# Tying the last slab's scans behind its neighbour's norm, and copying the gate's projection out of its bank

## The chip, the cores and the metric

The kernel runs on one core of a Trainium2 chip. A core has a matrix engine (TensorE, PE in the profile), a vector engine (VectorE, DVE), a scalar engine (ScalarE, ACT), a general engine (GpSimd, POOL), and queues that issue DMA transfers (SyncE, SP, issues nearly all of them here). Each engine works through its own instructions in order, and engines wait for one another by semaphores. Matrix results land in PSUM, here in banks of 128 x 512 f32. The metric is device time of one execution, in microseconds. Before the change the median of three runs was 1083.98 us (1078.87 to 1085.02).

## The reference

Four layers run one after the other on x, 32 sequences of 64 rows of 256 numbers: a cross attention (L0), two transformer blocks (L1 and L2: self attention, cross attention, MLP), and a recurrent layer (L3). The change touches L3 alone. Its core, cut:

```
xn = ln(x); sx = token_shift(xn)                 # row before minus this row
x5 = xn + sx * (maa_stack + tanh((xn + sx*maa_x) @ maa_w1) @ maa_w2)   # five mixes
w = exp(-exp(time_decay + tanh(x5[1] @ decay_w1) @ decay_w2))
r, k, v = x5[3] @ Wr.T, x5[0] @ Wk.T, x5[2] @ Wv.T
g = silu(x5[4] @ Wg.T)
step: a = k v^T; out = r (u*a + s); s = a + w*s   # scan over the 64 rows
att = group_norm(out) * gn_w + gn_b               # mean and variance over 8 numbers
x = x + (att * g) @ Wo.T
xn2 = ln(x); ...; x = x + sigmoid(xr @ ffn_Wr.T) * (square(relu(xk @ ffn_Wk.T)) @ ffn_Wv.T)
```

## The kernel before

The rows stand in four groups of 512 (`NG`); x stays in SBUF as four tiles `x0` to `x3`. Every layer is written as a list of small Python closures ("pieces"), each with a due time; `emit` sorts the pieces of all lists by due time and runs them. That gives a priority to each instruction. A scheduler then lays out the five engines' orders, with a timeline of its own, from these priorities and from the buffers that come free. So the order on an engine isn't written by hand, and a small edit can move instructions that it doesn't name.

The recurrent layer works in eight slabs of 256 rows (`recurrent(n)`, n = 0 to 7, names ending in r0 to r7). The second half of L2's MLP (`mlp_half`, L556, names with L2m) is spread between the first slabs. A slab has three lists:

- `first`: layer norm and shift (`norm`, L619), the five mixes (`mix`, L676: PE into `px5`, DVE L689, POOL adds at L692), then projections. `project` (L700) takes a bank of the tag "mm", of which there are two, and fills it with four matmuls (eight in the profile's records): `pv` for values, `pr` for receptance (L729 copies it out), `pk` for keys (L736 multiplies it by the receptance into `rk`, a tile with one buffer), `pg` for the gate. `own_term` (L738) has PE read `rk` into `pcf`. `decay_b` leaves the decays in `wsh`.
- `second`: the recurrence, in two halves e = 0 and 1 of four columns each. `spread` (L721) has SP load the values, broadcast, into a 1 MB tile `vb`, from a ring of three buffers of the tag "big", which the MLP's `hT` shares. `outer` multiplies by the keys (DVE L782), `scan` (L794) runs four scans on DVE (L797), `read` multiplies by the receptance (DVE L782 again), `over_keys` sums on PE into `pa`. Then the group norm: `norm_a` (L813) adds the own term (L815), has PE average into `pgm`, subtracts the mean on DVE (L819, the centring) and squares on ACT (L821); `norm_b` (L823) has PE average the squares into `pgv`, takes Ln and Exp on ACT (L829, L830, each behind a table load), and four DVE instructions (L833, L834) apply the norm, the weights and the gate to `at`. `to_rows` multiplies by Wo into `pwo`, and L198 adds to x.
- `third`: layer norm (names with fr), mixes `xk` and `xr` (L652), `pkk`, `pfr` and `pfv` on PE, and the output.

The gate before the change: ACT takes tanh of the bank `pg` (L772), and DVE reads the same bank for the product (L773). So the bank is free when DVE has come to L773:

```
ps = project("Wg", st["x5", 4], "g")
nc.scalar.activation(gt, ps, AF.Tanh, scale=0.5)
nc.vector.scalar_tensor_tensor(gt, gt, 1.0, ps, ALU.add, ALU.mult)
```

Which instruction waits for which bank is fixed when the program is built. In this one, the first matmul of `pr` of slabs 1, 2, 3 and 4 waits for L773 of the slab before; those of slabs 5, 6 and 7 wait for ACT's copy of `pv` (L712).

Of the kernel before, what the change touches and what calls it, by code (L numbers as in the profile page):

```python
# [1 line left out]

# [16 lines left out]
ALU = mybir.AluOpType  # L19
# [4 lines left out]
P = 128  # L24
NG = 4
# [55 lines left out]
def tile_xattn_stack(ctx: ExitStack, tc: tile.TileContext, a: dict, out: bass.AP):  # L81
    nc = tc.nc
# [11 lines left out]
    def bank(name, tag="mm"):  # L94
        return psum.tile([P, 512], FP, tag=tag, name=name, bufs=BUFS[tag])
# [503 lines left out]

    RB, RR = GB // 2, GR // 2  # L600

    def recurrent(n, pool, c3):

        g, u = n // 2, n % 2
        t = f"r{n}"
        st = {}
        mine = slice(n * RB, (n + 1) * RB)

        def flat(ap):
            return ap.rearrange("p c b t -> p (c b t)")  # L610
# [5 lines left out]
        def tile_(name, bufs=2, shape=None, p=pool, tag=None):  # L616
            return p.tile(shape or [P, 2, RR], FP, tag=tag or name, name=f"{name}_{t}", bufs=bufs)

        def norm(key, scale, bias, tag, row_of_state):  # L619


            def evac(ps):
                xn = st[key] = pool.tile([P, 2, RR], FP, tag=key, bufs=2, name=f"xn_{tag}")
                for c in range(2):
                    nc.scalar.activation(
                        xn[:, c], ps[:, c], AF.Identity, bias=vec(bias, c), scale=vec(scale, c),
                    )

            def evac_step(ps):
                sx = st["d" + key] = pool.tile([P, 2, RB, S], FP, tag="d" + key, name=f"sx_{tag}", bufs=2)  # L630
                for c in range(2):
                    nc.scalar.activation(
                        sx[:, c].rearrange("p b t -> p (b t)"), ps[:, c], AF.Identity,
                        bias=tiny[:, 2:3], scale=vec(scale, c),
                    )
                nc.gpsimd.tensor_tensor(
                    sx[:, :, :, 0], c3["st01"][:, :, mine, row_of_state],
                    st[key].rearrange("p c (b t) -> p c b t", b=RB)[:, :, :, 0], ALU.subtract,
                )

            layernorm_T(
                6 if key == "x" else 7, g, u, tag, evac, None, "tp" if key == "fx" else "sc", "n" + key, pool, 1,
                (c3["step"], evac_step),
            )
# [55 lines left out]
        def project(w, x, name, tag="mm"):  # L700
            ps = both(f"p{name}_{t}", tag)
            for o in range(2):
                project_T(ps[:, o], c3[w], slice(o * P, (o + 1) * P), x)
            return ps
# [63 lines left out]
        def gate():  # L768

            gt = st["gt"] = tile_("gt")  # L770
            ps = project("Wg", st["x5", 4], "g")
            nc.scalar.activation(gt, ps, AF.Tanh, scale=0.5)  # L772
            nc.vector.scalar_tensor_tensor(gt, gt, 1.0, ps, ALU.add, ALU.mult)  # L773

        first = [(0.5, lambda: norm("x", "L3_ln1_w", "L3_ln1_b", t, 1)), (0.0, first_mix), (1.2, maa)]
        first += [(0.85, lambda: mix(2, 3)), (1.7, vals), (0.85, lambda: mix(0, 1)), (1.7, recept), (1.7, keys)]
# [16 lines left out]

        def scan(e):  # L794
            v = st["vb", e].rearrange("p d c t -> p d (c t)")
            for d in range(4):
                nc.vector.tensor_tensor_scan(v[:, d], flat(st["wsh"]), v[:, d], 0.0, ALU.mult, ALU.add)  # L797
            if e == 1:
                st["wdone"]()

# [12 lines left out]
        def norm_a():  # L813
            at = st["at"] = tile_("at")
            nc.vector.tensor_tensor(at, st["own"], st["pa"], ALU.add)  # L815
            ps = bank(f"pgm_{t}", "pc")[:, :RR]
            for c in range(2):
                nc.tensor.matmul(ps, c3["avg"], at[:, c], start=(c == 0), stop=(c == 1))
            nc.vector.tensor_tensor(at, at, ps.unsqueeze(1).broadcast_to([P, 2, RR]), ALU.subtract)  # L819
            st["sq"] = tile_("sq", 1)  # L820
            nc.scalar.activation(st["sq"], at, AF.Square)  # L821

        def norm_b():  # L823
            at, sq = st["at"], st["sq"]
            ps = bank(f"pgv_{t}", "pc")[:, :RR]
            for c in range(2):
                nc.tensor.matmul(ps, c3["avg"], sq[:, c], start=(c == 0), stop=(c == 1))

            nc.scalar.activation(ps, ps, AF.Ln, bias=tiny[:, 1:2])  # L829
            nc.scalar.activation(ps, ps, AF.Exp, scale=-0.5)  # L830
            gnh = c3["gnh"]
            for c in range(2):
                nc.vector.scalar_tensor_tensor(at[:, c], at[:, c], gnh[:, c : c + 1], ps, ALU.mult, ALU.mult)  # L833
                nc.vector.scalar_tensor_tensor(  # L834
                    at[:, c], at[:, c], gnh[:, 2 + c : 3 + c], st["gt"][:, c], ALU.add, ALU.mult
                )

        def to_rows(src, w, done, name):
            def part(v):
                if v == 0:  # L840
                    st[name] = bank(f"p{name}_{t}", "pc" if w == "Wo" else "tp").rearrange("p (j n) -> p j n", j=2)
                for c in range(2):
                    nc.tensor.matmul(  # L843
                        st[name][:, v], src()[:, c, v * P : (v + 1) * P], c3[w][:, c],
                        start=(c == 0), stop=(c == 1),
                    )
                if v == 1:
                    done(st[name])

            return [(0.85, lambda v=v: part(v)) for v in range(2)]  # L850

        second = []
# [38 lines left out]
        third = [(0.5, ff_norm), (0.0, ff_mix), (1.7, ff_key)]  # L891
        third += to_rows(lambda: st["xr"], "ffn_Wr", done_r, "fr")
        third += to_rows(lambda: st["kk"], "ffn_Wv", done_v, "fv")
        return first, second, third


    wts, c3 = {}, {}
# [20 lines left out]
    with tc.tile_pool(name="lw", bufs=1) as wp, tc.tile_pool(name="lp", bufs=2) as pool:  # L918
# [148 lines left out]
        def loads(pieces, t0, t1):  # L1067
            return timed([(1.0, p) for p in pieces], t0, t1)

        plan = [timed(layer0(pool), *L0_AT), loads(load_self("L1"), L0_LOAD, L0_LOAD + 2.0)]  # L1070
        late = []
        for i, L in enumerate(("L1", "L2")):
            for k in range(2):
                for g in range(NG):
# [5 lines left out]
                    at = (8 + GAP) * i + 4 * k + g  # L1080
# [4 lines left out]
            at = (8 + GAP) * i + MLP  # L1085
# [17 lines left out]
    with tc.tile_pool(name="r", bufs=2, reuse_waits="tile") as pool:  # L1103
        def load(name, shape, src):
            load_to(pool, name, shape, src)

        def load_w(*names):
            for n in names:
                load(n, [P, 2, E], a["w3"][W3[n]].rearrange("(c p) n -> p c n", p=P))

        def hold(tag, bufs=2, shape=None):
            pool.tile(shape or [P, 2, RR], FP, tag=tag, name=f"hold_{tag}", bufs=bufs)

        def shifted_ring(name):

            c3[name] = ring(pool, name, [P, 2, RB, S], 2, lambda t: nc.gpsimd.memset(t[:, :, :, 0], 0.0))

        hold("fx")
        hold("dfx")
        hold("x5", 3)  # L1120
        hold("nx", 1)
        shifted_ring("wsh")
        hold("xk")
        hold("xr")
        hold("kk")
        hold("x")
        hold("rr", 2, [P, 2, E])
        hold("dx")
        shifted_ring("vsh")
        hold("ta", 1, [P, RR + S])  # L1130
        hold("vT")
        hold("rT")
        hold("tb", 1, [XM, RR])
        hold("rk", 1)
        hold("dT", 1, [64, RR])
        selu = c3["selu"] = pool.tile([P, 2, P], FP, name="selu", bufs=1)
        load_w("Wg", "Wo", "ffn_Wk", "ffn_Wr", "ffn_Wv")
        load("s0", [P, 2, RS, B], a["s0"])
        hold("gt")
        hold("at")  # L1140
        hold("sq", 1)
        shifted_ring("ksh")
        hold("nfx", 1)
        for c in range(2):
            nc.vector.tensor_scalar(selu[:, c], c3["sel"][:, c], vec("L3_faaaa", c), None, ALU.mult)
        gnh = c3["gnh"] = pool.tile([P, 4], FP, name="gnh", bufs=1)
        for i, n in enumerate(("L3_gn_w", "L3_gn_b")):
            nc.vector.tensor_scalar(
                gnh[:, 2 * i : 2 * i + 2], vecs[:, VEC[n] : VEC[n] + 2], 0.5, None, ALU.mult
            )  # L1150
        r = [recurrent(n, pool, c3) for n in range(2 * NG)]
        plan = []
        for n, (first, second, third) in enumerate(r):
            at = n * SLOT + START
            plan += [timed(first[:1], at - LEAD, at - LEAD), timed(first[1:], at, at + R1_D)]
            at += R2
            plan += [timed(second, at, at + R2_D)]
            at += R2_D + F0
            plan += [timed(third[:1], at, at), timed(third[1:], at + F1, at + F1 + F1_D)]
        plan.append(late)  # L1160
        emit(*plan)
# [78 lines left out]
```

## Time and profile before

The profile is of one execution, which took 1080.68 us; its span, first instruction to last, is 1078.9 us. All times below count from the start of that span.

| what | value |
|---|---|
| median of three runs | 1083.98 us |
| profiled execution, its span | 1080.68 us, 1078.9 us |
| PE, DVE, ACT, POOL busy | 983.6, 806.2, 549.2, 532.2 us |
| mean granted TensorE clock | 0.962 |
| 750 to 900 us: PE, DVE, ACT busy of 150 | 132.7, 127.4, 69.9 us |
| 900 to 1025 us: PE, DVE, ACT busy of 125 | 114.3, 113.3, 57.5 us |
| 1025 to 1079 us: PE, DVE, ACT busy of 54 | 35.7, 33.2, 22.8 us |
| scans L797 in the recurrent layer | 64, 77.6 us, 1276 ns each |

The recurrent layer's gates run from 749 us (slab 0) to 1027 us (slab 7). A share of busy time is an average: what a change is worth is read where its instructions stand, from the waits there. The timeline has, for each engine, the start and length of instructions, in brackets how long the engine had been idle, and what ended that. "PEclk" is the granted clock of PE as a share of full speed.

### The profile page before, as it was taken

To read this page: it belongs to the slowest core of one execution; us is meant where nothing else is said; L and a number is where in the kernel's file an instruction comes from. 1 tells how busy PE (TensorE), PEld (TensorE's weight loads), DVE (VectorE), ACT (ScalarE), POOL (GpSimd) and SP (SyncE) were. 2 spreads that over 40 slices of the span, in tenths; PEclk is the share of its full clock that TensorE was granted. 3 is DMA by queue.
4 is the path that set the end of the run, shared out by engine and by line. 5 is a ranking of instruction groups with operands and counts; after the bars stand their busy time and mean duration, and the time that the engine had idled before them with its cause. 6 is when DMAs were issued, how large, how long until landed. Compare 5 with 4: busy or idle time off the path is not lost.

```text
span 1078.9 us, 26319 instructions
## 1 busy us (share of the span) xinstructions
PE 983.6 (91%) x10764; PEld 787.8 (73%) x10764; DVE 806.2 (75%) x1513; ACT 549.2 (51%) x1271; POOL 532.2 (49%) x552
## 2 busy tenths in 40 slices
PE   8998999899989999989989999898989898988966
PEld 4886776667778989877767778787768677765645
DVE  5864688878877654777787887647887987999983
ACT  4743653554456644864454555454436464453334
POOL 4343766767657344756577665442434434153200
PEclk9999998999999999989899999999889999998889
DMA  9300111111100100140111101112122121332400
GB/s 301 105 21 21 23 45 32 38 25 27 26 22 7 40 1 21 46 138 22 41 39 28 26 21 32 31 36 66 41 70 60 50 61 40 95 76 69 98 11 29
DMA packets 45947, 53.39 MB, mean 49 GB/s; under 512 B 16146, under 2 KB 40068, under 8 KB 43780
## 3 DMA queue, kind: packets, MB, share of 16 engines
q1 hardware_dynamic: 40292, 49.60, 17.1%
q10 hardware_dynamic: 5536, 2.12, 0.8%
q8 instruction: 85, 1.39, 0.5%
q14 instruction: 34, 0.28, 0.1%
HBM read 38.83 MB, written 4.21 MB: 40 GB/s over the span
## 4 chain that ended last, share of the span: by engine, by line
PE 43%; DVE 32%; ACT 8%; POOL 8%; issue 4%; DMA 3%; SPq 0%; ACTq 0%; POOLq 0%; DVEq 0%
DVE vb_r L797 6%; PE pf_L1m L187 4%; PE pf_L2m L187 3%; DVE vb_r L782 3%; PE pfo_L1m L187 3%; POOL s_L2c L463 2%; DVE x L198 2%; POOL s_L1c L463 2%; PE pr L312 2%; PE pfo_L2m L187 2%; PE pwo_r L843 1%; PE px_r L132 1%; PE pq_L1c L187 1%; DVE s_L1c L458 1%; POOL s_L1s L463 1%
## 5 line engine op out<-in xcount | busy, mean ns | idle before, releaser
L692 POOL TENSOR_TENSOR x_r<-x_r,xn_r 128x512 f32<-128x512 f32 x40 | 63.6, 1604 | 113.7 <-DVE x_r L689 111.8
L797 DVE TENSOR_TENSOR_SCAN vb_r<-wsh,vb_r 128x512 f32<-128x512 f32 x64 | 77.6, 1276 | 5.6 <-ACT wsh L696 4.1
L463 POOL TENSOR_TENSOR s_L1s<-s_L1s,n 128x512 f32<-128x512 f32 x32 | 43.0, 1356 | 39.9 <-DVE s_L1s L458 39.2
L187 PE MATMUL pf_L2m<-lnT_L2m,w_L 128*128 128x256 f32 x384 | 57.8, 303 | 1.7 <-ACT vbd L430 0.7
L187 PEld LDWEIGHTS pf_L2m<-lnT_L2m,w_L 128*128 128x128 f32 x384 | 51.8, 202 | 7.6 <-issue 2.5
L187 PE MATMUL pfo_L2m<-w_L,hT_L2m 128*128 128x256 f32 x384 | 55.2, 291 | 1.5 <-DVE hT_L2m L581 1.5
L463 POOL TENSOR_TENSOR s_L2s<-s_L2s,n 128x512 f32<-128x512 f32 x32 | 43.0, 1360 | 26.9 <-DVE s_L2s L458 26.3
L187 PE MATMUL pfo_L1m<-w_L,hT_L1m 128*128 128x256 f32 x384 | 54.5, 288 | 1.6 <-POOL hT_L1m L580 0.8
L187 PE MATMUL pf_L1m<-lnT_L1m,w_L 128*128 128x256 f32 x384 | 51.9, 288 | 3.9 <-ACT hf_L1m L577 1.2
L463 POOL TENSOR_TENSOR s_L2c<-s_L2c,n_L2c 128x512 f32<-128x512 f32 x32 | 41.6, 1320 | 27.6 <-DVE s_L2c L458 26.7
L463 POOL TENSOR_TENSOR s_L1c<-s_L1c,n_L1c 128x512 f32<-128x512 f32 x32 | 41.3, 1309 | 25.8 <-DVE s_L1c L458 24.8
L187 PEld LDWEIGHTS pf_L1m<-lnT_L1m,w_L 128*128 128x128 f32 x384 | 47.5, 191 | 7.2 <-ACT hf_L1m L577 2.1
L187 PEld LDWEIGHTS pfo_L2m<-w_L,hT_L2m 128*128 128x128 f32 x384 | 48.7, 190 | 5.2 <-issue 2.7
L187 PEld LDWEIGHTS pfo_L1m<-w_L,hT_L1m 128*128 128x128 f32 x384 | 49.3, 191 | 3.4 <-POOL hT_L1m L580 1.0
L580 POOL TENSOR_SCALAR hT_L1m<-hf_L1m 128x512 fp32r<-128x512 f32 x32 | 21.8, 682 | 55.4 <-ACT hf_L1m L577 53.5
L577 ACT ACTIVATE hf_L1m<-pf_L1m,b_L 128x256 f32<-128x256 f32 x64 | 26.6, 471 | 42.3 <-PE pf_L1m L187 39.9
L581 DVE TENSOR_TENSOR hT_L1m<-hf_L1m,hT_L1m 128x512 fp32r<-128x512 f32 x32 | 25.3, 791 | 30.1 <-POOL hT_L1m L580 30.1
L581 DVE TENSOR_TENSOR hT_L2m<-hf_L2m,hT_L2m 128x512 fp32r<-128x512 f32 x32 | 24.7, 772 | 26.7 <-POOL hT_L2m L580 26.6
L580 POOL TENSOR_SCALAR hT_L2m<-hf_L2m 128x512 fp32r<-128x512 f32 x32 | 22.2, 694 | 40.1 <-ACT hf_L2m L577 39.8
L577 ACT ACTIVATE hf_L2m<-pf_L2m,b_L 128x256 f32<-128x256 f32 x64 | 26.6, 472 | 28.5 <-PE pf_L2m L187 23.0
L782 DVE TENSOR_TENSOR vb_r<-vb_r,ksh 128x2048 f32<-128x2048 f32 x16 | 38.3, 2409 | 2.7 <-DMA vb_r<-vd_r 2.7
L282 ACT ACTIVATE att<-pe,nmx 128x256 f32<-128x256 f32 x64 | 29.5, 476 | 19.3 <-DVE nmx L280 17.2
(388 smaller groups left out, 3062.1 us busy)
## 6 DMA issues: line engine op xcount, KB each, us to landing
vb_r<-vd_r SPq DMA_DIRECT2D x16, 1024.0 KB
raw_w_L<-in_L_w_dram SPq DMA_DIRECT2D x4, 1024.0 KB
y<-in_y_dram SPq DMA_DIRECT2D x8, 256.0 KB
x<-in_x_dram SPq DMA_DIRECT2D x8, 256.0 KB
ctxT_L1c<-in_yT_dram SPq DMA_DIRECT2D x4, 512.0 KB
kbd<-kT_L1s SPq DMA_DIRECT2D x64, 32.0 KB
kbd<-kT_L1c SPq DMA_DIRECT2D x64, 32.0 KB
kbd<-kT_L2s SPq DMA_DIRECT2D x64, 32.0 KB
```

Of the source, the lines that this page charges most:

```text
L132: return lambda: nc.tensor.matmul(ps, sta, mov, start=start, stop=stop)
L187: nc.tensor.matmul(ps, sta[x], mov[y], start=(at == 0), stop=(at == n - 1))
L198: nc.vector.tensor_tensor(xs, xs, ps, ALU.add)
L282: nc.scalar.activation(att[:, 2 * h + c, :], pe[:, c, :], AF.Exp, bias=nmx[:, h, c : c + 1], accum_out=rs[:, h, c : c + 1],)
L312: nc.tensor.matmul(pr[:, m, h, :], att[:, 2 * h + c, m * P : (m + 1) * P], xvT[:, c, h, :], start=(c == 0), stop=(c == 1),)
L463: nc.gpsimd.tensor_tensor(s[:, r], s[:, r], n(j).unsqueeze(1).broadcast_to([P, 8, S]), ALU.add)
L577: nc.scalar.activation(raw[:, i], ps[:, i], AF.Gelu_apprx_tanh, bias=w()["b1"][:, 2 * f2 + i : 2 * f2 + i + 1])
L580: nc.gpsimd.tensor_scalar(h[:, 0], raw, 1.0, 0.0, ALU.mult, ALU.add)
L581: nc.vector.tensor_tensor(h[:, 1], raw, h[:, 0], ALU.subtract)
L692: nc.gpsimd.tensor_tensor(d, d, st["x"], ALU.add)
L782: nc.vector.tensor_tensor(v, v, x.unsqueeze(1).broadcast_to([P, 4, 2 * RR]), ALU.mult)
L797: nc.vector.tensor_tensor_scan(v[:, d], flat(st["wsh"]), v[:, d], 0.0, ALU.mult, ALU.add)
```

## The change

Two edits in `recurrent`.

The gate: ACT, after its tanh, copies the bank `pg` into an SBUF tile `g`, and DVE's product reads `g`. The tile takes the one buffer of the tag "rk". Eight ACT copies of 128 x 512 f32 are added, one a slab; the DVE instructions stay, one operand from SBUF instead of PSUM.

The tie: for the last slab, n = 7, the four scans of half 0 are issued on DVE only after the centring (L819) of slab 6, and those of half 1 only after the last norm instruction (L834) of slab 6. `issue_after` fixes an order on one engine, without a semaphore. To do so, `recurrent` now gets the state of the slab ahead, and the slabs are built and planned one by one.

```diff
-    def recurrent(n, pool, c3):
+    def recurrent(n, pool, c3, prev):
...
             ps = project("Wg", st["x5", 4], "g")
             nc.scalar.activation(gt, ps, AF.Tanh, scale=0.5)
-            nc.vector.scalar_tensor_tensor(gt, gt, 1.0, ps, ALU.add, ALU.mult)
+
+            g_ = tile_("g", 1, tag="rk")
+            nc.scalar.copy(g_, ps)
+            nc.vector.scalar_tensor_tensor(gt, gt, 1.0, g_, ALU.add, ALU.mult)
...
         def scan(e):
             v = st["vb", e].rearrange("p d c t -> p d (c t)")
-            for d in range(4):
-                nc.vector.tensor_tensor_scan(v[:, d], flat(st["wsh"]), v[:, d], 0.0, ALU.mult, ALU.add)
+
+            with tc.issue_after(prev[("centred", "normed")[e]]) if n == 2 * NG - 1 else nullcontext():
+                for d in range(4):
+                    nc.vector.tensor_tensor_scan(v[:, d], flat(st["wsh"]), v[:, d], 0.0, ALU.mult, ALU.add)
...
-            nc.vector.tensor_tensor(at, at, ps.unsqueeze(1).broadcast_to([P, 2, RR]), ALU.subtract)
+            st["centred"] = nc.vector.tensor_tensor(
+                at, at, ps.unsqueeze(1).broadcast_to([P, 2, RR]), ALU.subtract
+            ).ins
...
-                nc.vector.scalar_tensor_tensor(
+                st["normed"] = nc.vector.scalar_tensor_tensor(
                     at[:, c], at[:, c], gnh[:, 2 + c : 3 + c], st["gt"][:, c], ALU.add, ALU.mult
-                )
+                ).ins
...
-        return first, second, third
+        return first, second, third, st
...
-        r = [recurrent(n, pool, c3) for n in range(2 * NG)]
-        plan = []
-        for n, (first, second, third) in enumerate(r):
+        plan, st = [], None
+        for n in range(2 * NG):
+            first, second, third, st = recurrent(n, pool, c3, st)
```

The two built programs can be laid side by side. Up to the gate of slab 0 they are the same. Behind it, besides the eight copies, these orders differ:

- PE: `pa` of slab 1's half 1 and the last part of `pwo` of slab 0 stand a little later among the MLP's matmuls; slab 2's `pw` comes before the transposes of fr0; `pa` of slab 4's half 1 comes before the first `px5` of slab 5 instead of after it; the tail is reordered.
- DVE: a few neighbours change places in slabs 0 to 2. In the tail, L819 of slab 6 comes before slab 7's first scans; then follow half 0's read and L833 and L834 of slab 6, and only then half 1's scans.
- ACT: the copies; slab 2's `dT` and `pw` come earlier among the norms; L821 of slab 6 comes before the tanh of slab 7.
- SP: the same order.
- `pr` of slabs 1 to 4 now waits for the copy on ACT instead of L773 on DVE; `pr` of slabs 5 to 7 waits for L712 as before.

## The prediction

> **What bounds the kernel now.** I read the page's shares first, then the chain of waits over slabs 0 to 2, PE's waits, the clock by stretches, and DVE's timeline at the end.
>
> ```profile
> PE 983.6 (91%) x10764; PEld 787.8 (73%) x10764; DVE 806.2 (75%) x1513; ACT 549.2 (51%) x1271; POOL 532.2 (49%) x552
> PE 43%; DVE 32%; ACT 8%; POOL 8%; issue 4%; DMA 3%; SPq 0%; ACTq 0%; POOLq 0%; DVEq 0%
> ```
>
> PE is the fullest engine, but in the recurrent layer the chain that sets the end (second line) changes between PE and DVE. The chain from 755 us shows how:
>
> ```profile
> 755.21 0.36 DVE gt_r L773
> ...
> 756.02 3.75 PE pr_r L192 x8
> 759.77 2.00 PE px_r L132 x4
> 761.77 2.87 PE pf_L2m L187 x12
> ...
> 766.98 1.97 PE pk_r L192 x8
> 768.95 1.43 PE pf_L2m L187 x12
> 770.37 1.04 PE pa_r L132 x16
> ...
> 771.47 7.23 DMA vb_r<-vd_r
> ...
> 778.72 2.30 DVE vb_r L782
> ...
> 799.37 0.69 DVE gt_r L773
> ...
> 800.19 2.05 PE pr_r L192 x4
> ```
>
> DVE's gate product L773 releases the bank, PE's `pr` of the next slab starts, and all behind it follows, to the load of the next `vb`, which waits for the end of `pa`. The reader should see that L773 stands on the chain only since PE waits for its bank. PE's waits give the price:
>
> ```profile
> PE pr_r L192 <- DVE gt_r L773: 6.6, 2, 3.4
> PE pr_r L192 <- DVE mv_L2m L147: 3.3, 1, 3.3
> ```
>
> 9.9 us in three waits (the second line is slab 0's: the small instruction after L773 is named, but the build has `pr` wait for L773). The fourth, `pr` of slab 4 at 889.99, was not held. PE pays again after the idle time; the column ahead of the DMA share is the granted clock:
>
> ```profile
> 756.00:760.00 4.00, 3.98 (x9) 2.82 (x10) 4.00 (x8) 0.19 (x1) 3.83 (x5) 0.50 0.01 2
> 800.00:804.00 4.00, 3.81 (x12) 2.65 (x16) 4.00 (x7) 0.02 (x1) 0.00 (x0) 0.50 0.00 0
> 846.00:850.00 4.00, 4.00 (x24) 2.14 (x24) 4.00 (x7) 0.58 (x1) 0.30 (x1) 0.64 0.00 0
> 943.00:947.00 4.00, 4.00 (x12) 3.00 (x12) 2.55 (x6) 0.00 (x0) 2.49 (x2) 0.61 1.04 225
> ```
>
> `pr` takes 3.75, 3.75 and 2.57 us there against 1.89 at full clock. Last, DVE in the tail (start, length):
>
> ```profile
> 1025.59 9.02 DVE L797 TENSOR_TENSOR_SCAN vb_r<-wsh,vb_r 128x512 f32<-128x512 f32 x8
> ...
> 1034.59 0.66 DVE L819 TENSOR_TENSOR at_r<-at_r,pgm_r 128x512 f32<-128x512 f32 x1
> ...
> 1035.82 4.49 DVE L782 TENSOR_TENSOR vb_r<-vb_r,rT_r 128x2048 f32<-128x2048 f32 x2
> ...
> 1049.62 0.69 DVE L819 TENSOR_TENSOR at_r<-at_r,pgm_r 128x512 f32<-128x512 f32 x1 [0.20 <-PE pgm_r L818]
> ...
> 1056.85 0.87 DVE L833 SCALAR_TENSOR_TENSOR at_r<-at_r,gnh,pgv_r 128x256 f32<-128x256 f32 x2 [6.41 <-ACT pgv_r L830]
> ```
>
> Eight scans run while the centring of slab 6 is ready (its mean was done at 1025.1); PE idles 8.89 us meanwhile; later DVE idles 6.41 us on slab 7's Exp.
>
> **The change part by part.** Line numbers are those of before.
>
> *Copies.* A copy of the same shape from a bank (L712) takes 0.58 us and holds ACT's queue about 0.5. Eight are 4.0 us of ACT. At slabs 0, 3, 5, 6 and 7 ACT idled 1.06, 2.41, 0.98, 2.86 and 7.58 us behind the tanh, so the copy is hidden; without that cover each would cost 0.5. At slab 2 the Ln behind it, its tables, the Exp and the cast shift by 0.5; the Exp (done 844.5) was awaited at 847.87: hidden. Slab 1: only the cast for the MLP shifts, done 799.0 instead of 798.5, first read after 801. Slab 4 is costed below. L773 from SBUF: the all-SBUF L885 takes 0.68, L773 0.67, so 0.
>
> *Slab 0's gate.* The copy ends near 750.2, so `pr` of slab 1 can follow `pa` at 752.7 (before: 756.02) and ends at 754.6. Next `px5` waits for DVE's L689, done about 756.7, then 1.1 us; PE's 24 MLP matmuls start near 758.0 (before: 761.70, then 4.67 us). Half clock may still hold there: at 4.67 us they end by 762.7, and `pk` and the next 12 (1.97 and 1.78 us) by 766.5. So `pa` of slab 0's half 1, which needs DVE's read, is bound by that read: 764.93 + 2.2 = 767.1. It ends at 768.3 instead of 771.37. The `vb` load on SP goes 3.1 us earlier, lands (7.2 us) at 775.6, and DVE, which before idled 2.75 us for it, is free from about 772.7, its waits for the MLP's halves being gone. Gain 3.0; bounds 1.5 (PE at half clock through `pk` and `pf`, some 1.6 us more) and 3.2.
>
> *Slab 1's gate.* Here ACT's tanh itself stands behind Ln and Exp with their tables; it starts at 797.44, the copy ends at 798.5, `pr` starts 1.6 us earlier than 800.19. If PE stays at full clock it is 1.9 long, the next `pa` follows DVE's read at 802.25 (before: 803.88), and the first 12 MLP matmuls end 3.15 earlier. With half clock over two stretches as in 799.6 to 806.4, only 1.3 of it is left. DVE's idle 4.44 us before 811.01 shrinks by as much. I take 2.3, near the middle, since PE still has a gap here (1.65 us, and again some 0.3 before the read).
>
> *Slab 2's gate.* `pr` moves from 845.90 to 842.5, but what is queued behind it on PE, `pa`, needs DVE's read, which ends at 847.87. So 3.4 us of idle time moves behind `pr`. `pa` starts 0.46 earlier, and the MLP matmuls can start when DVE's L179 is done at 850.9 instead of 851.75: 0.85 and, rounded up for `pf`, 1.0 at most. With the clock down over `pf` it costs 0.4. I take a gain of 0.4.
>
> *Slab 3's gate:* `pr` was not held: 0.
>
> *Slab 4's gate.* The copy delays ACT's L625 and L632 by 0.5, and PE now has `pa` (which needs the read of 938.45 to 940.66) ahead of the first `px5`, which ran at 939.70. So `pwo` of slab 3 starts at 943.95 instead of 942.96. DVE's L198 waited 1.45 us for it. If `pwo` again takes 3.54 us, the loss is 1.0; at 1.89 us DVE's own L689 (1.65 us from 944.0) sets it, 0.7 earlier than before. I take a loss of 0.5, nearer to the former, since the gap before is longer.
>
> *The tie.* Tail times by the after order and the durations of before: L819 of slab 6 ends at 1026.3, half 0's scans (4 x 1.12) at 1030.8, gate product 1031.4, read (2.2) 1033.7, L833 and L834 1035.2, half 1's scans 1039.7, `xk` and `xr` of fr5 1041.3, read 1043.5 (before: 1040.2). That is 3.3 us later for slab 7's last read. But before, its path behind the read stood in line on PE after `pwo`, `pfv` and `pkk` (1043.38 to 1048.56); now these are done early, and behind `pa` (1044.7) stand only `pfr` and `pgm`. L819 of slab 7 ends at 1048.5 instead of 1050.2. The norm of fr6, the squares, two table loads (1.28 each), Ln and Exp follow on ACT to 1055.1 (before: 1056.8), L834 1057.3, `pwo` 1059.2, add and statistics at 1060.5 (before: 1062.4). From there the order is the same: 1.9 us gained, if the clock holds. It won't quite: `pkk` and `pfr` of slab 6, which filled PE at 1060.00 to 1063.6, are done early, so PE idles about 3.3 us before the last transposes. After idle times of 3.39 and 3.21 us the rows above show 1.55 us (`pr` 2.57 + `pa` 1.94 against 1.89 + 1.07) and 2.7 us lost. I take 1.4, as PE has a short wait there. Tail: a gain of 0.5; bounds a gain of 1.9 and a loss of 0.6.
>
> A rule to weigh against these rows: the Trainium skill, "TensorE: Matmul & The Clock Gate", section "Part 1: The HAM clock gate", has the clock halve after at least one idle window of about 3.4 us. By it the new 3.3 us gap would mostly cost nothing, and the sum below would be a gain of 7.1. The trace is stricter: 943 to 947 shows 0.61 after an idle time of only 1.08 us and narrow matmuls. I go by the rows.
>
> *Sum:* 3.0 + 2.3 + 0.4 - 0.5 + 0.5 = 5.7 us. Against the profiled execution: span 1078.9 to 1073.2, time 1080.68 to 1075.0. That execution is 3.3 us under the median of the runs, 1083.98, whose own spread is 6 us; from the median it is 1078.3. I count from the middle of both, 1082.3, and say 1077. All lower bounds: 1.5 + 1.3 - 0.4 - 1.0 - 0.6 = 0.8 gained; all upper: 3.2 + 3.15 + 1.0 + 0.7 + 1.9 = 9.95.
>
> **The rivals.**
>
> *The wait only moves.* PE, let go by the gate, stops at the next DVE result, as at slab 2, everywhere. For it: at slabs 0 and 1, too, `pa` needs a DVE read that ends at 767.1 and 802.2. Against it: at slab 0 `pa` ran 3.2 us after that read was done, and slab 1's only 1.6 after. Then slab 0 gives its lower end and the rest nothing: about 1 us of 1082.3, 1081.
>
> *The clock comes back.* With 9.9 us of idle gone, PE stays at full clock at 756 to 766 and 800 to 806, and the tail holds too. For it: in both stretches the half clock followed the wait. Against it: gaps of 1.6 to 3.4 us remain. All upper bounds: 1082.3 - 9.95, 1072.
>
> *ScalarE takes DVE's place* (slower). PE then waits for the copy instead of L773, and each copy pushes ACT's later work. Price: 8 x 0.5 = 4.0 us on 1082.3, 1086, if nothing is won. It decides where ACT is late by more than the margin between copy and L773: 5.6 us at slab 0, 1.5 at slab 1, 4.1 at slab 2. Only slab 1's is near, as its tanh waits behind two table loads; and five of the eight copies have idle time behind them.
>
> That the change doesn't do what it says is excluded: the built order has the copies, the new waits and the tied scans.
>
> **How the numbers follow.** About 0.5% (5.4 us) is what a measurement of this kernel tells from no change. Forecast 0.48 (1077, its own range 1073 to 1081), the wait moves 0.22, the clock comes back 0.20, ScalarE 0.10. The forecast lies just beyond the 0.5% edge, so it gives 0.29 to faster and 0.19 to same; the clock case is faster, the moved wait is same, and of the ScalarE case (4.0 us, short of 5.4) two thirds are put to slower for what else would then be late. Faster 0.49, same 0.44, slower 0.07. The range reaches from 1070 (all upper bounds from the lower base) to 1084 (nothing won).
>
> **What would show it.** Right: `pr` of slab 1 near 752.7 behind `pa`, no wait of PE on the gate; the `vb` load of slab 1 issued near 768.4; DVE's wait before 811 cut to about 2; `pa` of slab 2's half 1 still waiting for DVE; L819 of slab 7 near 1048.5 less what was won before; a half-clock stretch on the last transposes. Wrong: half clock persisting at 756 to 766, a load of `vb` that lands later than 7.2 us, or PE waiting for the copy at slab 1 beyond 800.

## The result and the profile after

Over twelve executions each, the changed kernel took 1088.65 us (median; 1082.46 to 1092.07) and the kernel before 1083.61 us (1078.87 to 1087.85). The ratio is 1.0051, with a 95% interval of 1.0029 to 1.0073: 3 to 8 us slower. I had forecast 1077 us and a range of 1070 to 1084.

The profiled execution took 1089.29 us, its span is 1087.5 us. Page of the kernel after: busy times, and the chain that ended last by engine.

```profile
PE 988.3 (91%) x10764; PEld 791.6 (73%) x10764; DVE 805.6 (74%) x1513; ACT 553.9 (51%) x1279; POOL 532.5 (49%) x552
...
PE 42%; DVE 32%; POOL 9%; ACT 7%; issue 4%; DMA 3%; SPq 2%; ACTq 0%; DVEq 0%; POOLq 0%
```

The sums hardly move: ACT has 4.7 us more (the eight copies), PE 4.7 us more with the same instructions. One warning ahead of any comparison: the two programs are the same up to slab 0's gate, and yet the first scan of slab 0 starts at 744.28 us in one profile and at 748.25 us in the other. Those 3.97 us belong to the two executions, not to the change. So I compare lengths of stretches, not times of day.

PE's waits between 750 and 960 us (total us, how often, longest), kernel after:

```profile
PE pa_r L132 <- DVE vb_r L785: 9.1, 4, 3.6
PE pf_L2m L187 <- ACT hf_L2m L577: 3.3, 2, 2.1
PE pr_r L192 <- issue: 2.8, 2, 1.9
PE px_r L132 <- DVE x_r L689: 2.7, 2, 2.2
```

The same lines of the kernel before (the 9.9 us of `pr` stand in the prediction):

```profile
PE pa_r L132 <- DVE vb_r L782: 3.3, 2, 2.3
...
PE pk_r L192 <- ACT hf_L2m L577: 0.6, 1, 0.6
PE px_r L132 <- DVE x_r L689: 0.5, 1, 0.5
```

The 9.9 us in which `pr` waited for DVE are gone, as meant. But `pa` waits 9.1 us for DVE's read where it waited 3.3, `px` 2.7 for DVE where it waited 0.5, `pf` 3.3 for ACT, for which only `pk` had waited, 0.6. PE's idle time was moved behind `pr`, not removed.

What that does is seen at slab 2's gate. PE's timeline there (start, length, in brackets idle time ahead and its cause), first after:

```profile
843.95 1.89 PE L192 MATMUL pr_r<-x_r,Wr 128*128 128x256 f32 x8
849.45 1.94 PE L132 MATMUL pa_r<-vb_r,sel 128*32 128x256 f32 x16 [3.61 <-DVE vb_r L785]
851.31 0.58 PE L187 MATMUL pf_L2m<-lnT_L2m,w_L 128*128 128x256 f32 x1
851.82 2.07 PE L132 MATMUL px_r<-tb_r,mw2b 32*128 32x256 f32 x4
853.83 4.82 PE L187 MATMUL pf_L2m<-lnT_L2m,w_L 128*128 128x256 f32 x21
```

And the kernel before:

```profile
845.90 2.57 PE L192 MATMUL pr_r<-x_r,Wr 128*128 128x256 f32 x8 [3.39 <-DVE gt_r L773]
848.41 1.94 PE L132 MATMUL pa_r<-vb_r,sel 128*32 128x256 f32 x16
850.27 0.49 PE L187 MATMUL pf_L2m<-lnT_L2m,w_L 128*128 128x256 f32 x1
850.70 1.13 PE L132 MATMUL px_r<-tb_r,mw2b 32*128 32x256 f32 x4
851.75 2.78 PE L187 MATMUL pf_L2m<-lnT_L2m,w_L 128*128 128x256 f32 x21
```

The order on PE is the same. `pr` runs at full clock now (1.89 us), but `px` takes 2.07 us instead of 1.13 and the 21 MLP matmuls 4.82 instead of 2.78: 3.0 us more, back to back. They are on the path: in the chain that ended last, PE alone holds the stretch from 849.45 to 863.8 us. The granted clock says why. Windows of 3.41 us (window, length, PE busy and its matmuls, granted clock, DMA share, GB/s), after:

```profile
844.83:848.24 3.41, 1.01 (x5) 1.00 0.00 0
848.24:851.65 3.41, 2.21 (x17) 0.50 0.00 0
851.65:855.07 3.42, 3.42 (x11) 0.50 0.73 182
855.07:858.48 3.41, 3.41 (x18) 0.50 0.58 125
858.48:861.89 3.41, 3.41 (x18) 1.00 0.02 5
```

Before:

```profile
843.71:847.12 3.41, 1.22 (x6) 1.00 0.00 0
847.12:850.53 3.41, 3.41 (x21) 0.50 0.00 0
850.53:853.95 3.42, 3.42 (x23) 1.00 0.68 170
```

The clock is halved for whole stretches of 3.41 us, on a grid: in the profile of before four of them begin at 754.96, 799.33, 847.12 and 898.32 us, which is 13, 14 and 15 times 3.413 us apart. Here the halved stretch follows one with 1.22 us of PE work before and 1.01 after. Before, `pr` stood behind the idle time: the first halved stretch was busy throughout, with the rest of `pr` (to 848.5) and `pa`, and one was enough. After, `pr` stands ahead of the idle time; the first stretch is a third idle, the second holds `px`, which uses 32 rows of the array, and only the third is filled with full-size matmuls and is the last.

### The profile page after: what moved, and what is told of

It is laid out like the page before. It is cut to its first block, busy times and chain, and to the rows that moved or that the text cites. A ratio compares the mean times of both kernels' runs of the same rounds, so it can differ in the third digit from the quotient of the medians.

```text
span 1087.5 us, 26328 instructions
## 1 busy us (share of the span) xinstructions
PE 988.3 (91%) x10764; PEld 791.6 (73%) x10764; DVE 805.6 (74%) x1513; ACT 553.9 (51%) x1279; POOL 532.5 (49%) x552
## 3 DMA queue, kind: packets, MB, share of 16 engines
q10 hardware_dynamic: 5536, 2.12, 0.8%
## 4 chain that ended last, share of the span: by engine, by line
PE 42%; DVE 32%; POOL 9%; ACT 7%; issue 4%; DMA 3%; SPq 2%; ACTq 0%; DVEq 0%; POOLq 0%
DVE vb_r L802 7%; PE pf_L1m L187 4%; PE pf_L2m L187 3%; DVE vb_r L785 3%; PE pfo_L1m L187 3%; POOL s_L2c L463 2%; SPq L403 2%; POOL s_L1c L463 2%; DVE x L198 2%; PE pr L312 2%; POOL s_L1s L463 2%; PE pfo_L2m L187 2%; PE px_r L132 2%; PE pk_r L192 1%; PE pwo_r L850 1%
## 5 line engine op out<-in xcount | busy, mean ns | idle before, releaser
L692 POOL TENSOR_TENSOR x_r<-x_r,xn_r 128x512 f32<-128x512 f32 x40 | 66.2, 1670 | 116.9 <-DVE x_r L689 104.1
L187 PE MATMUL pf_L2m<-lnT_L2m,w_L 128*128 128x256 f32 x384 | 60.1, 310 | 6.0 <-ACT hf_L2m L577 3.7
L187 PE MATMUL pf_L1m<-lnT_L1m,w_L 128*128 128x256 f32 x384 | 51.9, 288 | 3.9 <-ACT hf_L1m L577 1.2
L581 DVE TENSOR_TENSOR hT_L1m<-hf_L1m,hT_L1m 128x512 fp32r<-128x512 f32 x32 | 25.3, 790 | 30.2 <-POOL hT_L1m L580 30.1
L581 DVE TENSOR_TENSOR hT_L2m<-hf_L2m,hT_L2m 128x512 fp32r<-128x512 f32 x32 | 24.7, 771 | 27.3 <-POOL hT_L2m L580 27.2
L282 ACT ACTIVATE att<-pe,nmx 128x256 f32<-128x256 f32 x64 | 29.6, 484 | 19.0 <-DVE nmx L280 16.3
```

The costliest lines, as they stand in the source:

```text
L187: nc.tensor.matmul(ps, sta[x], mov[y], start=(at == 0), stop=(at == n - 1))
L282: nc.scalar.activation(att[:, 2 * h + c, :], pe[:, c, :], AF.Exp, bias=nmx[:, h, c : c + 1], accum_out=rs[:, h, c : c + 1],)
L581: nc.vector.tensor_tensor(h[:, 1], raw, h[:, 0], ALU.subtract)
L692: nc.gpsimd.tensor_tensor(d, d, st["x"], ALU.add)
```

## The experiments

Edits are against the kernel after. "Tie off" is this, in `scan`, so that no scan is tied:

```diff
-            with tc.issue_after(prev[("centred", "normed")[e]]) if n == 2 * NG - 1 else nullcontext():
+            with tc.issue_after(prev[("centred", "normed")[e]]) if n == 2 * NG - 1 and e in () else nullcontext():
```

"Copy at SLABS" is this, in `gate`; DVE's product reads the bank at the other slabs:

```diff
-            g_ = tile_("g", 1, tag="rk")
-            nc.scalar.copy(g_, ps)
+            g_ = ps
+            if n in SLABS:
+                g_ = tile_("g", 1, tag="rk")
+                nc.scalar.copy(g_, ps)
```

The built orders show that these parts are independent: without the tie the tail has the order of before, without the copies all ahead of the tail has it.

**1. All copies, tie off.**

> All eight copies, no tie (the scans of slab 7 stand as before the change). Theory 'moved idle': the copies win 2 to 3 us at the gates of slabs 0 and 1 and lose 2.7 at slab 2, 1.0 in slab 3 and 2.9 at slab 4, because PE's idle time now stands ahead of narrow matmuls and the half clock lasts longer: 3 to 4.5 us slower than before, 1087. Rival 'the tie': the tail costs it all: no slower than before, 1082 to 1084. Rival 'ScalarE's time': eight copies of 0.5 us each on the path: 4 us slower, the same as the first theory here, to be told apart by the two runs with fewer copies.

1088.76 us against 1082.22 us: 1.0053 (1.0033 to 1.0074). The copies carry the whole loss.

**2. The tie alone** (copy at no slab: `if n in ():`).

> The tie alone, no copy. Theory 'moved idle': the tail costs 0 to 1.5 us (0.6 in the two profiles): 1083.5 to 1085. Rival 'the tie': the whole loss, 5 us: 1088.5. Rival 'ScalarE's time': no change.

1084.77 us against 1082.22: 1.0011 (0.9989 to 1.0032). The tie alone doesn't account for the loss; a cost of up to 3.5 us isn't excluded.

**3. Copies at slabs 0 and 1, tie off** (`if n in (0, 1):`).

> Copies at slabs 0 and 1 only, no tie. Theory 'moved idle': only the two gates that win are left: 2 to 3 us faster than before, 1081. Rival 'the tie': the same as all copies. Rival 'ScalarE's time': two copies, 1 us slower than before, 1084.6.

1083.43 us against 1082.22: 1.0008 (0.9988 to 1.0027). Neither theory's number: no loss, but the 2 to 3 us that slabs 0 and 1 should win aren't there.

**4. Copies at all but slabs 2 and 4, tie off** (`if n in (0, 1, 3, 5, 6, 7):`).

> Copies at slabs 0, 1, 3, 5, 6 and 7, no tie: slabs 2 and 4 read the bank on DVE as before the change. Theory 'moved idle': as fast as the copies at slabs 0 and 1 alone, 1081 (1.5 to 3 us faster than before), since the bank of slabs 5 to 7 is waited for by nobody on time and slab 3's pr was not held; the half clock ahead of slab 3's pa may still cost 1 us. Rival 'ScalarE's time': six copies of 0.5 us, 3 us slower than before, 1086.6.

1083.72 us: 1.0009 (0.9988 to 1.0031). With six copies the kernel isn't measurably slower, against 1.0053 with eight; nor is it faster, as I had expected. By the medians it isn't ScalarE's time, though the 3 us of that rival (1.0028) still lie inside the interval; the seventh run settles it. What costs should sit at slab 2 or 4.

**5. to 7. Slab 2 against slab 4, tie off:** all copies but slab 2's (`if n in (0, 1, 3, 4, 5, 6, 7):`), all but slab 4's (`if n in (0, 1, 2, 3, 5, 6, 7):`), and slab 2's alone (`if n in (2,):`).

> All copies but slab 2's, no tie. Theory 'slab 2': its copy alone costs (the clock stays halved for three stretches of 3.41 us instead of one at 848 us, and the next drop at 900 us lasts two instead of one): 1082.5 to 1084.5, one half-clock stretch at 848 to 852. Rival 'slab 4' (the copy delays ScalarE ahead of two transposes' evictions, and PE's order there changes): as slow as all copies, 1088. Rival 'both': 1085.5.

> All copies but slab 4's, no tie. Theory 'slab 2': as slow as all copies, 1087 to 1089. Rival 'slab 4': 1083. Rival 'both': 1085.5.

> The copy at slab 2 alone, no tie. Theory 'slab 2': the whole loss of the copies, 1086.5 to 1088.5 (4 to 6 us over before), three half-clock stretches from 848 us. Rival 'slab 4': 1082 to 1083. Rival 'ScalarE's time': one copy, 0.5 us.

Against 1082.76 us: without slab 2's copy 1085.80, 1.0023 (1.0000 to 1.0046); without slab 4's 1090.39, 1.0062 (1.0042 to 1.0083); with slab 2's alone 1087.58, 1.0041 (1.0020 to 1.0061). Slab 2's copy by itself makes most of the loss, 4 us where ScalarE's time for one copy would make 0.5, and leaving out slab 4's brings nothing back. The fifth run lies above the 1084.5 that I had allowed, but its interval reaches it; by itself it would fit "both" (1085.5) as well, which the sixth, at 1090.39, does not. In the traces the seventh run's orders on PE, DVE and POOL are those of before from slab 0's scans to 990 us, and ACT's has the one copy more: nothing but the copy was changed.

**8. Idle matmuls in slab 2's gap,** all copies, tie off. In `over_keys`, ahead of the sums of half 1:

```diff
             v = st["vb", e]
+            if e == 1:
+                for _ in range({2: 8}.get(n, 0)):
+                    nc.tensor.matmul(st["pa"][:, e], c3["avg"], st["own"][:, 0], start=True, stop=True)
```

> All copies, no tie, and eight idle matmuls of the group norm's average (128 x 256, their result overwritten) for PE between pr of slab 3 and pa of slab 2's half 1, six of them in the gap of 3.6 us that the copy left there. They change the planned order behind that place somewhat. Theory 'the clock': with the gap filled the half-clock stretches at 848 to 858 us are gone or one is left, pa takes 1.1 us instead of 1.9 and the next 23 MLP matmuls 3.5 instead of 4.8; from pa to hT of the MLP 1.8 us shorter; 1085 if nothing else moves. Rival 'the wait on DVE': the same time from pa to hT as without the idle matmuls, at whatever clock; 1088 or later, as PE has 3 us more to do.

1085.33 us against 1082.76: 1.0035 (1.0007 to 1.0063). PE's timeline in this run:

```profile
842.34 2.75 PE L815 MATMUL pa_r<-vT_r,avg 128*128 128x256 f32 x12
845.24 1.07 PE L132 MATMUL pa_r<-vb_r,sel 128*32 128x256 f32 x16
846.24 0.38 PE L187 MATMUL pf_L2m<-lnT_L2m,w_L 128*128 128x256 f32 x1
846.81 1.13 PE L132 MATMUL px_r<-tb_r,mw2b 32*128 32x256 f32 x4 [0.19 <-DVE x_r L689]
848.58 0.70 PE L856 MATMUL pwo_r<-Wo,at_r 128*128 128x256 f32 x2 [0.65 <-DVE at_r L847]
849.99 2.17 PE L856 MATMUL pwo_r<-Wo,at_r 128*128 128x256 f32 x6 [0.70 <-DVE at_r L847]
851.59 4.28 PE L187 MATMUL pf_L2m<-lnT_L2m,w_L 128*128 128x256 f32 x23
```

With the gap filled, `pa` and `px` run at full clock (1.07 and 1.13 us instead of 1.94 and 2.07): that part of the theory holds. But the planner answered the added matmuls with another order, `pwo` now waits twice for DVE ahead of `pf`, and one halved stretch falls on `pf` after all (850.8 to 854.2). From that `pa` to the MLP's next `hT` on DVE (L581) it takes 12.15 us, against 10.05 with all copies and no idle matmuls in the first run, where I had expected 1.8 us less. So the total, close to the 1085 of the theory, doesn't speak for it, and what the clock alone is worth can't be read from it.

**9. to 11. Idle matmuls in the gaps of before,** tie off, six a slab: at slab 2 with copies at slabs 0 and 1 (`{2: 6}`), at slab 0 with no copy (`{0: 6}`), at slabs 0, 1 and 2 with no copy (`{0: 6, 1: 6, 2: 6}`). In `over_keys`, behind the sums of half 0:

```diff
+            if e == 0:
+                for _ in range({2: 6}.get(n, 0)):
+                    nc.tensor.matmul(st["pa"][:, 1], c3["avg"], st["rT"][:, 0], start=True, stop=True)
```

> Copies at slabs 0 and 1 only, no tie, as in the third run, and six idle matmuls (the group norm's average on the receptance, 128 x 256, their result overwritten) in PE's gap of 3.3 us at slab 2's gate, ahead of the pr of slab 3 that waits for DVE. Theory 'the clock': pr 1.9 us instead of 2.6, pa 1.1 instead of 1.9, no half-clock stretch at 848; 1.5 us or more gained from slab 2's last read to slab 3's scans, the stretch at 900 gone or as it was; 1081 to 1083. Rival 'the wait on DVE': 0 gained there.

> The kernel before with six idle matmuls in PE's gap of 3.3 us at slab 0's gate, ahead of the pr of slab 1. Theory 'the clock': none or one half-clock stretch at 755 to 765 where the profile of before has three; slab 1's first scans 2 us sooner after slab 0's than there (37.1 us); as fast as before or up to 2 us faster, 1081 to 1083. If the gain of the copy at slab 0 was the bank and not the clock, the idle matmuls win nothing: 37.1 us stay.

> The kernel before with six idle matmuls at each of the gates of slabs 0, 1 and 2; the planned order behind them changes. Theory 'the clock': at most one half-clock stretch at each of the three gates, against 3, 2 and 1 before; 1078 to 1083. Rival: PE's 9 us of idle matmuls run into its other work, and the half clock costs nothing where DVE sets the pace: 1085 to 1090.

Against 1084.24 us: 1086.35, 1.0025 (1.0006 to 1.0044); 1091.41, 1.0077 (1.0047 to 1.0107); 1092.26, 1.0080 (1.0050 to 1.0111). All three are slower, so no better version came of it. PE in the ninth run, slab 2's gate:

```profile
844.71 2.75 PE L824 MATMUL pa_r<-rT_r,avg 128*128 128x256 f32 x12
848.09 1.97 PE L192 MATMUL pr_r<-x_r,Wr 128*128 128x256 f32 x8 [0.63 <-DVE gt_r L778]
850.25 1.07 PE L132 MATMUL pa_r<-vb_r,sel 128*32 128x256 f32 x16 [0.19 <-issue]
851.77 1.13 PE L132 MATMUL px_r<-tb_r,mw2b 32*128 32x256 f32 x4 [0.45 <-DVE x_r L689]
853.15 0.86 PE L187 MATMUL pf_L2m<-lnT_L2m,w_L 128*128 128x256 f32 x5 [0.25 <-DVE lnT_L2m L179]
853.85 0.60 PE L858 MATMUL pwo_r<-Wo,at_r 128*128 128x256 f32 x2
854.97 1.56 PE L858 MATMUL pwo_r<-Wo,at_r 128*128 128x256 f32 x6 [0.52 <-DVE at_r L849]
```

No stretch is halved at 848, `pr` and `pa` are at full clock, and most of what they save turns into waits for DVE behind `pr` (0.45, 0.25, 0.52 us; the 0.63 ahead of it is what is left of the gap). From slab 2's last read to slab 3's first scan it takes 29.6 us, against 27.5 in the third run, as the planned order behind the gap changed too. The expectation of 1.5 us gained was wrong. The waits suggest that DVE sets the pace over the one halved stretch; as the order changed, that isn't shown. In the tenth run `pr` at slab 0 is at full clock too (1.97 us), and then the new order makes PE wait elsewhere:

```profile
759.76 3.14 PE L187 MATMUL pf_L2m<-lnT_L2m,w_L 128*128 128x256 f32 x24
768.38 3.75 PE L192 MATMUL pk_r<-x_r,Wk 128*128 128x256 f32 x8 [5.48 <-ACT hf_L2m L577]
```

`pk` now stands behind all 24 MLP matmuls and waits 5.48 us, and the halved stretches fall there.

**12. The copy at slab 0 alone,** tie off (`if n in (0,):`; PE's order is that of before).

> The copy at slab 0 alone, no tie; PE's order is that of the kernel before. So far the profiles show one half-clock stretch at slab 0's gate with the copy (six of six) and 3, 1 and 3 without. Theory 'the clock': one stretch again, slab 1's first scans 35.1 us after slab 0's (37.1 in the profile of before), slab 1's gate as before with two stretches; 1 to 2 us faster than before, 1081 to 1082.5. Rival 'nothing is won at slab 0 but by chance': 1083, and two or three stretches at times.

1081.94 us against 1081.95: 0.9998 (0.9979 to 1.0017). No gain is measured; one of up to 2 us isn't excluded.

**13. and 14. The kernels before and after, unchanged, once more,** for their profiles.

> The kernel before, unchanged, once more, for its half-clock stretches at the gates. If slab 4's loss in the profile after was chance, the stretches at 943 to 957 us are 0, 1 or 3 again without any copy, and slab 2's gate shows one. If it was the copy, slab 4's gate shows one here.

> The kernel after, unchanged, once more. Theory 'slab 2': three half-clock stretches from 848 us and two from 900 us again, whatever the other gates show; slab 3's first scans 2.7 us later after slab 2's last read than before, the next MLP product 1.0 us more.

1080.92 and 1086.74 us, one execution each. The fourteenth came as expected at slab 2: three halved stretches and then two, 30.25 us where before has 27.56, and 31.44 for the next product where before has 30.39. The profile of before again, slab 0's gate:

```profile
755.07 3.65 PE L192 MATMUL pr_r<-x_r,Wr 128*128 128x256 f32 x8 [3.26 <-DVE mv_L2m L147]
758.65 1.13 PE L132 MATMUL px_r<-tb_r,mw2b 32*128 32x256 f32 x4
759.71 3.13 PE L187 MATMUL pf_L2m<-lnT_L2m,w_L 128*128 128x256 f32 x24
```

The same program, the same wait of 3.26 us; but `px` and `pf` take 1.13 and 3.13 us, not 2.07 and 4.67 as in the profile that I predicted from. The grid makes the difference: here the halved stretch begins 0.09 us behind the start of `pr`, is filled by it, and is the only one; there it began 1.06 us ahead of `pr`, and two more followed, with `px` in the second. With the copy (profile after) it is the other way round:

```profile
756.65 1.99 PE L192 MATMUL pr_r<-x_r,Wr 128*128 128x256 f32 x8
760.81 1.13 PE L132 MATMUL px_r<-tb_r,mw2b 32*128 32x256 f32 x4 [2.17 <-DVE x_r L689]
761.87 4.82 PE L187 MATMUL pf_L2m<-lnT_L2m,w_L 128*128 128x256 f32 x24
766.69 1.97 PE L192 MATMUL pk_r<-x_r,Wk 128*128 128x256 f32 x8
770.77 1.69 PE L187 MATMUL pf_L2m<-lnT_L2m,w_L 128*128 128x256 f32 x12 [2.12 <-ACT hf_L2m L577]
```

**All profiles together.** The table has the lengths in us, from DVE's timelines, with the number of halved stretches on PE in brackets. "Slab 0" runs from the first scan of slab 0 to the first of slab 1; "slab 1" on to the read of slab 2's half 1; "slab 2" on to the first scan of slab 3; "slab 3" on to DVE's L581 behind the next MLP product; "slab 4" from the own-term add of slab 4 to the first scan of slab 5; "tail" from the own-term add of slab 6 to the end. A star marks a gate with the copy, or the tie. The parts between, not shown, are 39.20 to 39.23 and 64.16 to 64.20 us in all twelve. The four runs with idle matmuls, whose order is another, are left out.

| profile | slab 0 | slab 1 | slab 2 | slab 3 | slab 4 | tail |
|---|---|---|---|---|---|---|
| before | 37.12 (3) | 64.27 (2) | 27.56 (1) | 30.39 (1) | 15.42 (1) | 56.45 |
| before, again | 34.91 (1) | 64.54 (2) | 27.58 (1) | 30.67 (1) | 18.30 (3) | 56.39 |
| tie alone | 34.86 (1) | 64.67 (2) | 27.58 (1) | 30.60 (1) | 18.30 (3) | 57.11* |
| copy at 2 | 37.18 (3) | 64.38 (2) | 30.44* (3) | 31.41 (2) | 18.31 (3) | 55.12 |
| copy at 0 | 35.13* (1) | 64.38 (2) | 27.58 (1) | 30.88 (1) | 16.77 (2) | 55.19 |
| copy at 0, 1 | 35.15* (1) | 66.23* (3) | 27.51 (1) | 30.25 (1) | 13.90 (0) | 55.38 |
| copy at all but 2, 4 | 35.14* (1) | 66.03* (3) | 27.58 (1) | 30.56* (1) | 18.29 (3) | 55.35 |
| copy at all but 2 | 35.42* (1) | 63.74* (1) | 27.58 (1) | 30.56* (1) | 18.30* (3) | 55.41 |
| all copies | 35.14* (1) | 66.18* (3) | 30.42* (3) | 31.42* (2) | 15.44* (1) | 57.81 |
| copy at all but 4 | 35.39* (1) | 63.44* (1) | 30.24* (3) | 31.42* (2) | 18.30 (3) | 58.29 |
| after | 35.16* (1) | 63.69* (1) | 30.24* (3) | 31.42* (2) | 18.31* (3) | 57.02* |
| after, again | 36.83* (1) | 62.68* (1) | 30.25* (3) | 31.44* (2) | 18.31* (3) | 57.08* |

Slab 2 is the one gate where the copy decides: 27.57 us on average without, 30.32 with, 2.75 us, and no profile crosses over. Nor is it the place of the grid: from the start of slab 2's last read to the grid's next boundary it is 0.90 to 1.58 us in the seven without, all with one halved stretch, and 1.13 to 1.57 us in the five with, all with three. The product behind it ("slab 3") takes 0.86 us more in the same five profiles, two halved stretches instead of one, whether or not slab 3's gate has the copy. At slab 1 the copy makes 62.7 to 63.7 or 66.0 to 66.2 us, as the stretches fall, on average 64.57 against 64.45: nothing. At slab 0 it is 35.42 against 36.02: 0.6 won, all of it from the two profiles without the copy that had three halved stretches; there the grid does differ (counted from slab 0's first scan, the boundaries lie 0.44 and 0.72 us behind a multiple of 3.413 us in the two with three, 1.59 and 1.71 in the two with one). Slab 4 is 13.9, 15.4, 16.8 or 18.3 us with none, one, two or three of them; one and three are found with the copy and without, so these runs show no effect of the copy there. The tail takes 57.0 to 57.1 us with the tie and 55.1 to 58.3 without.

By these averages the change costs 2.75 + 0.86 + 0.4 (slab 4) + 0.9 (tail) + 0.1 - 0.6 = 4.4 us; 5.0 were measured. Only the first two terms, 3.6 us, are shown; the others are within what one program shows from run to run.

The traces also tell which halved stretch is the last. In the recurrent layer (730 us on) of all sixteen profiles, PE was busy throughout in 150 halved stretches. 106 of them had under 0.9 us of matmuls on 32 rows, such as `px`, and none was followed by another halved one; 40 had over 1.2 us, and all were; of the 4 between, 3 were. (Many are the same few places of the program, profile after profile.) Matmuls on 32 columns, such as `pa`, don't do that: of 31 with over 1.5 us of them, 2 were followed. So the 2.07 us of `px` in the second halved stretch go with the third, and the `pa` in the one stretch of before did no harm. No run changed `px` alone.

## Why the prediction was wrong

*What bounds the kernel.* Right: the path changes between PE and DVE, and `pr` did wait for the bank alone.

*Copies at no cost.* Right but for slab 1, as far as the runs tell. ScalarE's 4.7 us are hidden by the medians; six copies cost nothing that can be measured. At slab 1, `pr` waits for the copy itself (the copy ends at 800.82 us, `pr` starts at 800.92), as reckoned.

*Slab 0, a gain of 3.0.* The steps came nearly as written: `pr` right behind `pa`, a halved `pf` of 4.82 us (I had kept 4.67). The load of `vb` came later than reckoned, as the 12 MLP matmuls ahead of `pa` waited 2.12 us for ScalarE, which my chain left out. In this pair of profiles 2.0 us were won. The step that failed is the price of the state before: the 37.1 us that I took from one profile are 34.9 in another profile of the same program, with the bank's wait in place. I counted three halved stretches as the kernel's, and they were that execution's. Worth over all profiles: 0.6, under my lower bound of 1.5.

*Slab 1, a gain of 2.3.* `pr` started earlier, as reckoned, but at half clock, since PE's idle time stayed around it. The bound that I had set for half clock over two stretches, 1.3, was not the worst case: three stretches occur and lose 1.7 against the mean without the copy. The mean gain is nothing.

*Slab 2, a gain of 0.4, bounds -0.4 to 1.0.* This is the step that failed and decided the sign. I wrote that 3.4 us of idle time move behind `pr`, and they did (3.61). Then I priced a clock that is down over `pf` at 0.4. It lasts for three stretches instead of one, `px` and `pf` take 3.0 us longer, and with the next product 3.6 us are lost. I had a row for it in hand, `pf` at 4.67 us for 24 in slab 0's stretch, where twice the 1.70 for 12 at full clock make 3.4, and didn't ask which instruction would stand first behind the moved gap.

*Slab 4, a loss of 0.5.* In the first pair of profiles the loss is 2.9, but the repeats show 18.3 us without the copy as well. Not shown to be the change; that the mean over all profiles, 0.4, is near my 0.5 is luck.

*The tail, a gain of 0.5.* The centring of slab 7 ended at 1056.67, which is 1048.6 on the clock of before (8.03 us off in this stage): 1.7 us sooner, as reckoned. Then two things took it back. DVE and PE, after:

```profile
1055.99 0.68 DVE L824 TENSOR_TENSOR at_r<-at_r,pgm_r 128x512 f32<-128x512 f32 x1
...
1063.25 0.87 DVE L840 SCALAR_TENSOR_TENSOR at_r<-at_r,gnh,pgv_r 128x256 f32<-128x256 f32 x2 [1.47 <-ACT pgv_r L837]
1064.04 0.68 DVE L891 SCALAR_TENSOR_TENSOR rr_r<-rr_r,pfv_r 128x512 f32<-128x512 f32 x1
```

```profile
1064.77 1.99 PE L850 MATMUL pfr_r<-ffn_Wr,xr_r 128*128 128x256 f32 x8 [1.98 <-DVE rr_r L891]
1066.60 1.89 PE L850 MATMUL pwo_r<-Wo,at_r 128*128 128x256 f32 x8
...
1074.31 3.27 PE L850 MATMUL pfv_r<-ffn_Wv,kk_r 128*128 128x256 f32 x8 [0.24 <-ACT xn_fr L625]
```

I had `pfr` of slab 6 done early. It waits 1.98 us for the bank that DVE's L891 frees, and L891 stands on DVE behind slab 7's L840; so `pwo` of slab 7 comes behind `pfr`, at 1066.60 (1058.57 on the clock of before, where it had started at 1058.17). And the half clock after the last gap, for which I took 1.4, is there: `pfv` takes 3.27 us instead of 1.99, 1.3 us. In this pair the tail loses 0.6, the lower bound; over all profiles it is 0.9, not clear of what the tail shows without the tie.

*The sum.* From the 5.7 us forecast to the 4.4 lost it is 10.1 us: slab 2 with the next product makes 4.0 of them, slab 0 and slab 1 2.4 each, the tail 1.4. The gains that weren't there took the forecast to about nothing, and slab 2 made it a loss.

*The rivals.* "The wait only moves" named the mechanism that the waits show; it was priced as a gain of 1 us, since I let the moved wait cost nothing. "ScalarE takes DVE's place" had the sign but not the cause: six copies without a measurable loss and one copy that costs 4 us speak against it. "The clock comes back" fails at slab 2, where the copy brings three halved stretches for one; at slab 0 all eight profiles with the copy have one, but two of the four without have one as well.

*A rule and the rows.* The Trainium skill, "TensorE: Matmul & The Clock Gate", section "Part 1: The HAM clock gate", has an activity window of about 3.4 us that runs freely and doesn't start with the kernel. The profiles agree: halved stretches of 3.41 us and multiples of it, on a grid that lies elsewhere in each execution. I cited the section for when the clock halves and left out that it is a grid; at slab 0 the place of the grid goes with three stretches or one, so that one profile of a gap is a sample and not a price. To go by the rows and not by an idle window was right: `pfv` in the tail ran at half clock.

What stays open: that 32-row matmuls keep the clock down is read from where they stand in the traces, and no run tested it alone. Nor could the gap at slab 2 be filled without the planner changing the order, so the clock's share of the 2.75 us rests on the lengths of the same instructions in the same order, not on a run that restores the clock alone.

## What to carry to other kernels

Freeing a producer's bank earlier doesn't remove a wait if the next instruction in the queue needs the same late engine: look at what will stand first behind the moved gap, and whether it can run at the clock that the gap leaves. Here a large projection right behind the idle time was worth more than the same projection ahead of it, where a 32-row matmul came to stand behind the gap. Where a stage's length depends on the granted clock, take its price from several profiles of one program before a few microseconds are forecast from it.

## What the runs showed of the hardware that I had not expected

- The granted clock of PE changes on a grid of 3.41 us, and from slab 0 on halved times come as one, two or three such stretches. The window ahead of a halved one need not be idle: 1.22 and 1.01 us of PE work in 3.41 us went before the two at slab 2.
- One program without any edit takes 34.9 or 37.1 us from slab 0's scans to slab 1's, and 15.4 or 18.3 us at slab 4's gate, with one or three of these stretches. Together that is as much as the change itself makes.
- In a halved stretch, matmuls on 32 rows went with another halved one (40 of 40 with over 1.2 us of them, none of 106 with under 0.9), and matmuls on 32 columns didn't.
- Idle matmuls kept the clock up where they stood (`pr` 1.97 us instead of 2.44, `pa` 1.07 instead of 1.94), and each of the four kernels that had them was slower than the kernel before, by 2 to 8 us between the medians.
